# Layer 0's graph convolution in pairs of groups: four tiled mixes in a row, then the full products of two groups

## The chip, the cores and the metric

The kernel runs on one core of one Trainium2 chip. Its engines are TensorE (PE in the profile: matmuls; PEld are its weight loads), VectorE (DVE), ScalarE (ACT), GpSimd (POOL) and SyncE (SP), which issues most DMAs; each works through its own queue in order. Matmul results land in PSUM, which has eight banks here, and VectorE or ScalarE must copy them out. The metric is the device time of one execution in microseconds (us), lower is better.

## The reference, cut to what matters

Four layers, each of them `x = x + layer(relu(layernorm(x)))`, on x of 128 batches, 64 nodes and 256 features in f32; the same 64 x 64 adjacency serves all. Layer 0, which the change touches, is a graph convolution of two steps followed by LSTMs over windows of nodes:

```python
h = relu(layernorm(x))                                        # kernel's "h"
h = relu(einsum('ts,bsh->bth', adj, h @ Wg0 + bg0))           # first step
h = relu(einsum('ts,bsh->bth', adj, h @ Wg1 + bg1))           # second step
for p in range(1, 5):                                         # LSTM p over windows of p nodes
    ...
```

The layers after it (attention, a batch-normalized network, three graph products) are not changed.

## The kernel before

**Groups.** The 8192 rows (128 batches x 64 nodes) are cut into 16 groups of 512 rows (`NG`, `GN`): 4 tiles of 128 partitions, and each tile holds two batches of 64 nodes. Every group passes four stages in layer 0. Each step first mixes the nodes with the adjacency and then multiplies by the weights; the bias goes through the adjacency's row sums.

- `first_mix(g)`, line 427: the normalization of group g (`ln_relu`, line 117: statistics L92, L94 and L95 on VectorE, a power L96 on POOL, one more L98 on VectorE, whose result is called nmr, and then four activations L111 on ScalarE write h); then `mix` (line 132), 32 matmuls of 64 x 64 (L144), which address the array as four tiles of 64 x 64. They fill two PSUM banks, and VectorE copies both to m0 (L157 and L452). `copied_of[g]` (line 425) remembers the second copy.
- `first_weights(m0)`, line 479: 8 full matmuls of 128 x 256 (L487) into two banks. For each bank VectorE adds the bias (L495) and POOL takes the relu (L496); the result is h1.
- `second_mix(h1)`, line 499: again 32 tiled matmuls (L144) into two banks; ScalarE copies both to m1 (L157).
- `second_weights(g, m1)`, line 504: 4 full matmuls of 128 x 512 (L511) into two banks; VectorE adds the bias (L516), ScalarE takes the relu (L519) and writes into `hs`, which the LSTMs read.

The profile counts each f32 matmul twice: a mix is x64, a first weights x16, a second weights x8.

**Order of the stages (lines 522 to 532).** One loop, software-pipelined: in turn g it issues the first mix of g, the second weights of g-2, the second mix of g-1 and the first weights of g. So on TensorE a mix always stands between two stages of full products, except at the two ends of the loop. At the end, the second weights of group 14 are split around the second mix of 15.

**What sets the order on the other engines.** The program is written stage by stage, and a scheduler merges the engines' instructions by what they wait for. `tc.issue_after(...)` holds an instruction behind another one in the program. In `first_mix` it holds the normalization of group g behind `copied_of[g - 2]` (line 447), and `ln_relu` gets a function, `lambda: copied_of[g - 1]` (line 448), that holds its last small operation L98 behind the copy of the group before. Other work is hung on the same list: sums of LSTM weights (L226) and differences of finished groups (L214) behind `copied_of[5]` to `copied_of[15]`, and the forms of the adjacency (L374 to L397) behind the mix of group 4.

**Buffers.** All PSUM tiles come from one ring of eight banks (`psp`, line 47). h, m0, h1, m1 and s1 have two buffers each (`gp`, line 321). The groups from 4 on load x into three buffers (line 445) through SP's queue, which also carries the LSTM weights of 1 MB each (L318).

**After the loop** the LSTMs start on TensorE (L568) with products of 128 x 256, of which the first read groups 0 to 7.

Of the kernel before, what the change touches and what calls it, by code (L numbers as in the profile page):

```python
# [20 lines left out]
NG = NTOK // GN  # L21
# [17 lines left out]
def adj_preln_kernel(ctx: ExitStack, tc: tile.TileContext, x_in, adj, vec, bg0, bg1,  # L39
# [9 lines left out]
    def bank(shape=(P, 512)):  # L49
        return psp.tile(list(shape), F32, tag="ps", name="ps")  # L50
# [6 lines left out]
    def load_x(x, g):  # L57
        nc.sync.dma_start(out=x, in_=x_view[:, g * GT : (g + 1) * GT, :])
# [25 lines left out]
    def ln_scale(src, between=None, n=GT, early=False):  # L84


        st = lnp.tile([P, GT, 6], F32, tag="st", name="st")[:, 0:n]
        mv = lnp.tile([P, GT, 2], F32, tag="mv", name="mv")[:, 0:n]
        rstd = lnp.tile([P, GT], F32, tag="rstd", name="rstd")[:, 0:n]
        nmr = lnp.tile([P, GT], F32, tag="nmr", name="nmr")[:, 0:n]  # L90
        for t in range(n):
            nc.vector.bn_stats(st[:, t, :], src[:, t, :])  # L92
        for t in range(n):
            nc.vector.bn_aggr(mv[:, t, :], st[:, t, :])  # L94
        var = nc.vector.tensor_scalar(rstd, mv[:, :, 1], LN_EPS, None, ALU.add)  # L95
        nc.gpsimd.tensor_tensor(out=rstd, in0=rstd, in1=mhalf[:, 0:n], op=ALU.pow)  # L96
        with tc.issue_after(between().ins) if between else nullcontext():
            last = nc.vector.scalar_tensor_tensor(nmr, mv[:, :, 0], -1.0, rstd, ALU.mult, ALU.mult)  # L98
        return rstd, nmr, (var if early else last).ins

    def ln_apply(src, dst, rstd, nmr, n=GT, on_vector=()):

        for t in range(n):
            if t in on_vector:
                nc.vector.tensor_scalar(
                    dst[:, t, :], src[:, t, :], rstd[:, t : t + 1], nmr[:, t : t + 1],
                    ALU.mult, ALU.add,
                )
                last = nc.vector.tensor_scalar(dst[:, t, :], dst[:, t, :], 0.0, None, ALU.max)
                continue  # L110
            last = nc.scalar.activation(  # L111
                dst[:, t, :], src[:, t, :], AF.Relu,
                bias=nmr[:, t : t + 1], scale=rstd[:, t : t + 1],
            )
        return last.ins

    def ln_relu(src, dst, between=None):

        rstd, nmr, _ = ln_scale(src, between)
        ln_apply(src, dst, rstd, nmr)  # L120
# [193 lines left out]
    with tc.tile_pool(name="lw", bufs=5) as lw:  # L314
# [6 lines left out]
        with tc.tile_pool(name="gw", bufs=1) as gw, tc.tile_pool(name="gcn", bufs=2) as gp, \  # L321
# [103 lines left out]
            copied_of = []  # L425

            def first_mix(g):
                nonlocal first_copied, first_scalar, turned, second_ln
                h = gp.tile([P, GT, D], F32, tag="h", name="h")
                if g == 0:  # L430
                    for k, (rstd, nmr, _) in enumerate(lns):
                        two = slice(2 * k, 2 * k + 2)
                        ln_apply(xs[0][:, two], h[:, two], rstd, nmr, 2, (1,) if k else ())
                elif g == 1:
                    with tc.issue_after(first_copied):
                        rstd, nmr, second_ln = ln_scale(xs[1])
                    with tc.issue_after(first_scalar):
                        ln_apply(xs[1], h, rstd, nmr)
                    with tc.issue_after(first_copied):
                        row_sums()  # L440
                else:
                    if g < NK:
                        x = xs[g]
                    else:
                        x = gp.tile([P, GT, D], F32, tag="x", name="x", bufs=3)
                        load_x(x, g)
                    with tc.issue_after(second_ln if g == 2 else copied_of[g - 2].ins):
                        ln_relu(x, h, lambda: copied_of[g - 1])
                m0 = gp.tile([P, 2, GN], F32, tag="m0", name="m0")

                def on_vector_last(*args):
                    copied_of.append(nc.vector.tensor_copy(*args))  # L452
                    return copied_of[-1]

                if g == 0:


                    def on_scalar_first(*args):
                        nonlocal first_scalar
                        last = nc.scalar.copy(*args)  # L460
                        first_scalar = last.ins
                        return last

                    copied = mix(h, adj2, 2, m0, (on_scalar_first, on_vector_last))
                    first_copied = copied
                    with tc.issue_after(copied):
                        nc.vector.tensor_scalar(rb0[:, 0, :], rb0[:, 0, :], rsum, None, ALU.mult)
                else:
                    copied = mix(h, adj2, 2, m0, (on_vector, on_vector_last))
                if g == NG // 4:  # L470

                    with tc.issue_after(copied):
                        adjacency_forms()
                        turned = normalized_adjacency()
                if g == NG // 2:
                    turned()
                return m0

            def first_weights(m0):

                h1 = gp.tile([P, GT, D], F32, tag="h1", name="h1")
                for k in range(2):
                    ps = bank((P, 2, D))
                    for t in range(2):
                        tok = (2 * k + t) * P
                        for c in range(2):
                            nc.tensor.matmul(  # L487
                                ps[:, t, :],
                                lhsT=m0[:, c, tok : tok + P],
                                rhs=wg[0][:, c, :],  # L490
                                start=(c == 0),
                                stop=(c == 1),
                            )
                    hk = h1[:, 2 * k : 2 * k + 2, :]
                    nc.vector.tensor_tensor(hk, ps, rb0.to_broadcast([P, 2, D]), ALU.add)  # L495
                    nc.gpsimd.tensor_scalar(hk, hk, 0.0, None, ALU.max)  # L496
                return h1

            def second_mix(h1, last):
                m1 = gp.tile([P, 2, GN], F32, tag="m1", name="m1")  # L500
                mix(h1, adj2, 2, m1, (on_scalar, on_vector if last else on_scalar))
                return m1

            def second_weights(g, m1, ms=range(2)):

                dst = hs[g // PER][:, :, :, (g % PER) * GB : (g % PER + 1) * GB]
                for m in ms:
                    ps = bank((P, GB, NODES))
                    pf = ps.rearrange("p b n -> p (b n)")
                    for c in range(2):  # L510
                        nc.tensor.matmul(  # L511
                            pf, lhsT=wg[1][:, c, m * P : (m + 1) * P], rhs=m1[:, c, :],
                            start=(c == 0), stop=(c == 1),
                        )
                    s1 = gp.tile([P, GB, NODES], F32, tag="s1", name="s1")
                    nc.vector.tensor_tensor(  # L516
                        s1, ps, rb1[:, m].to_broadcast([P, GB, NODES]), ALU.add
                    )
                    nc.scalar.activation(dst[:, m], s1.rearrange("p b n -> p n b"), AF.Relu)  # L519


            h1, m1 = None, None
            for g in range(NG + 2):
                if g < NG:
                    m0 = first_mix(g)
                before = m1
                if before is not None:
                    second_weights(g - 2, before, range(1 if g == NG else 2))
                m1 = second_mix(h1, g == NG) if h1 is not None else None
                if g == NG:  # L530
                    second_weights(g - 2, before, [1])
                h1 = first_weights(m0) if g < NG else None


        with tc.tile_pool(name="back", bufs=1, reuse_waits="tile") as back_pool, \
# [198 lines left out]
            for p, nk in ((1, 8), (2, 8), (3, 7), (4, 8)):  # L734
                n = nk * HB
# [6 lines left out]
                for j in range(0, len(units), 2):  # L742
# [23 lines left out]
                    for t in range(1, p):  # L766
                        for i, u in enumerate(two):
# [21 lines left out]
                            if p == 4 and j == 2 and t == p - 1 and i == 0:  # L789

                                h = back_pool.tile([P, GT, D], F32, tag="hc", name="h")
# [10 lines left out]
    def arena(pool):  # L802
        return pool.tile([P, 4, GN], F32, tag="arena", name="arena")
# [47 lines left out]
    with tc.tile_pool(name="att", bufs=2, reuse_waits="tile") as ap_:  # L851
# [151 lines left out]
        for g in range(NG):  # L1003
# [14 lines left out]
            if g == 0:  # L1018
                h = normalized(1)
# [51 lines left out]
            with tc.issue_after(sub):  # L1071
# [4 lines left out]
                if g + 2 < NG:  # L1076
                    h = normalized(g + 2)
# [493 lines left out]
    for g in range(NG + 1):  # L1571
        if g == 0:
            bring(0, 3)
        if g < NG:

            m1 = arena(ar_right)
            h1, summed = first_weights(a, m1)
# [89 lines left out]
```

## Time and profile before

| what | value |
|---|---|
| median of 4 runs | 2450.08 us (2449.26 to 2452.09) |
| the profiled execution | 2452.09 us, its span 2450.20 us |
| first matmul of the mix of group 2 | 22.92 us from the span's start |
| first matmul of the LSTMs (L568) | 163.85 us |
| TensorE in the stretch 20 to 140 us | busy 20.00 us of every 20 |
| VectorE there | 12.86 to 14.49 us of every 20 |
| ScalarE there | 10.06 to 12.56 us of every 20 |
| POOL there | 8.08 to 9.10 us of every 20 |
| granted TensorE clock, 20 us and later | 1.00 |

The profile is that of one execution. In the list of groups each row names line, engine, operation, what it writes and reads, the shape, the count, the busy time and the mean duration in ns, and after the last bar how long the engine stood idle before such instructions and who ended that. A timeline merges neighbours of one kind: start, duration of the whole row, engine, line, operation, the part of the array (64*64 or 128*128 for a matmul), shape, count. In both, `[a <-b]` says that the engine was idle for a us until b released it. The ends of matmuls are modelled and neighbours overlap by some hundredths to tenths of a us, so the pace of TensorE is read from one start to the next.

### The profile page before, as it was taken

The numbers are of one execution on the slowest core, as the hardware profiler recorded it, in microseconds if no ns is written. First come the engines' busy times: TensorE is split into PE (matmuls) and PEld (weight loads), VectorE is DVE, ScalarE is ACT, GpSimd is POOL, SyncE is SP. The second block draws the span as 40 slices with busy tenths as digits, with TensorE's granted clock in tenths as the row PEclk, the third lists the DMA queues.
The fourth block names the chain that finished last, engine by engine and source line by source line (L and its number), as shares of the span: only waits on it lengthen the run. The fifth ranks groups of instructions, "written<-read, shape, count | busy, mean of one in ns | idle before, by whom it ended". The sixth has DMA issues, their size and how long they took to land.

```text
span 2450.2 us, 46580 instructions
## 1 busy us (share of the span) xinstructions
PE 2429.6 (99%) x19564; PEld 2073.1 (85%) x19564; DVE 1541.3 (63%) x2768; ACT 1128.0 (46%) x2026; POOL 463.6 (19%) x400
## 2 busy tenths in 40 slices
PE   9999999999999999999999999999999999999999
PEld 6678888889999998888888864486988898898888
DVE  6668866656566575575698886476555445454544
ACT  4557754544445344353455566564333323333332
POOL 4432211111111111112234331023111111111110
PEclk9999999999999999999999999999999999999999
DMA  3200000001000000153246410010133100000000
GB/s 123 99 2 1 1 18 1 1 1 35 1 1 1 1 1 1 18 100 69 48 87 121 79 35 2 1 61 10 34 54 62 27 10 19 10 10 10 18 10 18
DMA packets 161586, 73.20 MB, mean 30 GB/s; under 512 B 104416, under 2 KB 157792, under 8 KB 161376
## 3 DMA queue, kind: packets, MB, share of 16 engines
q1 hardware_dynamic: 147712, 56.82, 9.4%
q0 software_dynamic: 12672, 12.58, 3.4%
q8 instruction: 154, 2.52, 0.4%
q10 hardware_dynamic: 992, 0.82, 0.1%
q14 instruction: 56, 0.46, 0.1%
HBM read 40.84 MB, written 20.97 MB: 25 GB/s over the span
## 4 chain that ended last, share of the span: by engine, by line
PE 90%; DVE 6%; ACT 3%; POOL 1%; issue 1%; DMA 0%; DVEq 0%; POOLq 0%; ACTq 0%
PE ps L568 41%; PE ps L1454 16%; PE ps L1502 8%; PE ps L830 4%; PE ps L144 4%; PE ps L880 3%; PE ps L1418 2%; PE ps L511 2%; PE ps L487 2%; PE ps L1210 2%; PE ps L1261 2%; PE ps L902 1%; ACT arena L237 1%; POOL arena L187 1%; PE ps L963 1%
## 5 line engine op out<-in xcount | busy, mean ns | idle before, releaser
L568 PE MATMUL ps<-diff,s 128*128 128x256 f32 (+1 forms) x1824 | 393.5, 371 | 0.9 <-DVE diff L689 0.9
L1454 PE MATMUL ps<-arena 128*128 128x256 f32 x1792 | 392.6, 381 | 0.0
L1454 PEld LDWEIGHTS ps<-arena 128*128 128x128 f32 x1792 | 337.9, 190 | 54.2 <-issue 9.5
L568 PEld LDWEIGHTS ps<-diff,s 128*128 128x128 f32 x1824 | 345.9, 190 | 33.8 <-issue 1.6
L582 ACT ACTIVATE gates<-gates,lbias 128x512 f32<-128x512 f32 (+5 forms) x426 | 244.2, 620 | 200.5 <-DVE gates L193 144.4
L187 POOL TENSOR_TENSOR gates<-p 128x512 f32<-128x512 f32 (+1 forms) x115 | 148.8, 1294 | 881.8 <-DVE p L183 831.0
L568 PE MATMUL ps<-h,w 128*128 128x256 f32 (+1 forms) x1028 | 241.0, 371 | 0.0
L568 PE MATMUL ps<-diff,w 128*128 128x256 f32 (+1 forms) x1040 | 238.7, 370 | 0.0
L568 PEld LDWEIGHTS ps<-diff,w 128*128 128x128 f32 x1040 | 197.4, 190 | 18.2
L568 PEld LDWEIGHTS ps<-h,w 128*128 128x128 f32 x1028 | 195.0, 190 | 19.2 <-issue 0.5
L582 ACT ACTIVATE gates<-ps,lbias 128x256 f32<-128x256 f32 (+3 forms) x213 | 91.8, 477 | 247.5 <-PE ps L568 247.4
L187 POOL TENSOR_TENSOR arena<-arena 128x256 f32<-128x256 f32 (+1 forms) x73 | 81.8, 1121 | 580.5 <-DVE arena L183 550.9
L237 ACT ACTIVATE arena<-arena 128x512 f32<-128x512 f32 (+1 forms) x160 | 88.6, 582 | 187.0 <-POOL arena L187 94.8
L1502 PE MATMUL ps<-arena 128*128 128x128 f32 x1280 | 149.7, 276 | 0.0
L193 DVE TENSOR_TENSOR gates<-p,ps 128x512 f32<-128x512 f32 (+1 forms) x115 | 76.3, 664 | 114.4 <-PE ps L568 114.2
L1502 PEld LDWEIGHTS ps<-arena 128*128 128x128 f32 x1280 | 145.5, 192 | 1.1
L193 DVE TENSOR_TENSOR arena<-arena,ps 128x256 f32<-128x256 f32 (+1 forms) x73 | 43.6, 597 | 156.0 <-PE ps L1454 87.4
L568 PE MATMUL ps<-state,w 128*128 128x256 f32 (+1 forms) x512 | 116.1, 370 | 0.9 <-ACT p L179 0.8
L182 DVE TENSOR_TENSOR p<-p,ps 128x512 f32<-128x512 f32 (+1 forms) x131 | 86.8, 663 | 47.9 <-PE ps L568 46.8
L197 DVE TENSOR_TENSOR gates<-p,ps 128x512 f32<-128x512 f32 (+1 forms) x115 | 76.6, 666 | 63.3 <-PE ps L568 62.7
L830 PE MATMUL ps<-arena,w 128*128 128x512 f32 x256 | 116.0, 606 | 0.0
L568 PE MATMUL ps<-state,s 128*128 128x256 f32 (+1 forms) x512 | 115.8, 369 | 0.0
(207 smaller groups left out, 4022.2 us busy)
## 6 DMA issues: line engine op xcount, KB each, us to landing
x<-in_x SPq DMA_DIRECT2D x19, 512.0 KB, 4.9
y<-turned SPq DMA_DIRECT2D x64, 128.0 KB, 3.7
v<-vt SPq DMA_DIRECT2D x128, 64.0 KB, 2.3
w<-in_wih SPq DMA_DIRECT2D x4, 1024.0 KB, 8.4
x_for_h<-in_x SPq DMA_DIRECT2D x8, 512.0 KB, 7.5
x<-y POOLq DMA_DIRECT2D x8, 512.0 KB, 6.1
x_for_h<-y POOLq DMA_DIRECT2D x8, 512.0 KB, 6.7
z<-w SPq DMA_DIRECT2D x64, 64.0 KB, 2.0
```

What stands on the lines that cost most here:

```text
L144: last = nc.tensor.matmul(pss[b][half * 64 : half * 64 + 64, c, t, :], lhsT=src[rows, t, col : col + 64], rhs=a2[rows, :], start=True, sto ...
L182: nc.vector.tensor_tensor(p1, p1, ps[2], ALU.add)
L187: nc.gpsimd.tensor_tensor(out=out[1][1], in0=p1, in1=p5, op=ALU.add).ins
L193: nc.vector.tensor_tensor(out[0][1], p1, ps[1], ALU.add)
L197: last = nc.vector.tensor_tensor(to, p, q, ALU.add)
L237: nc.scalar.activation(o, o, func)
L568: nc.tensor.matmul(ps[:, r], lhsT=wc[:, j, :], rhs=bc, start=first and r == 0 and c == 0, stop=True, skip_group_check=True,)
L582: nc.scalar.activation(o, ps, func, bias=lbias[:, col : col + 1])
L830: nc.tensor.matmul(ps, lhsT=w1[:, c, m * P : (m + 1) * P], rhs=a[:, 2 + c, :], start=(c == 0), stop=(c == 1),)
L880: nc.tensor.matmul(ps[:, r, :], lhsT=w[:, r * P : (r + 1) * P], rhs=x, start=first and r == 0, stop=True, skip_group_check=True,)
L1454: nc.tensor.matmul(ps[:, r, :], lhsT=w[:, c, col : col + P], rhs=b[:, c, :], start=first and r == 0 and c == 0, stop=c == 1, skip_group_ch ...
L1502: nc.tensor.matmul(ps[:, t, :], lhsT=w[:, c, t * P : (t + 1) * P], rhs=b[:, c, :], start=first and t == 0 and c == 0, stop=c == 3, skip_gr ...
```

## The change

Groups 2 to 15 are taken in pairs. For a pair g, g+1 the order is: first mix of g, second mix of g-2, first mix of g+1, second mix of g-1; then first weights of g, second weights of g-2, first weights of g+1, second weights of g-1. In the pair 14, 15 both first weights stand ahead of both second weights. So a second mix and its weights stand two groups behind, where they stood one and two. Groups 0 and 1 keep their order, the pair 2, 3 has no second mix of 0 (it is done before), and after the loop come the second mixes of 14 and 15 and then their second weights. `copied_of[g - 1 - g % 2]` makes L98 of an odd group wait for the copy of the pair before, not for that of its own pair's first group. The first of the two copies of m1 stays on ScalarE; the second goes to VectorE for groups 14 and 15, where it was for 15 alone.

```diff
--- before.py
+++ after.py
@@ -445,7 +445,7 @@
                         x = gp.tile([P, GT, D], F32, tag="x", name="x", bufs=3)
                         load_x(x, g)
                     with tc.issue_after(second_ln if g == 2 else copied_of[g - 2].ins):
-                        ln_relu(x, h, lambda: copied_of[g - 1])
+                        ln_relu(x, h, lambda: copied_of[g - 1 - g % 2])
                 m0 = gp.tile([P, 2, GN], F32, tag="m0", name="m0")
 
                 def on_vector_last(*args):
@@ -519,17 +519,36 @@
                     nc.scalar.activation(dst[:, m], s1.rearrange("p b n -> p n b"), AF.Relu)
 
 
-            h1, m1 = None, None
-            for g in range(NG + 2):
-                if g < NG:
-                    m0 = first_mix(g)
-                before = m1
-                if before is not None:
-                    second_weights(g - 2, before, range(1 if g == NG else 2))
-                m1 = second_mix(h1, g == NG) if h1 is not None else None
-                if g == NG:
-                    second_weights(g - 2, before, [1])
-                h1 = first_weights(m0) if g < NG else None
+            h1_of, m1_of = [], []
+
+            def first_weights_of(m0):
+                h1_of.append(first_weights(m0))
+
+            def second_mix_of(g):
+                m1_of.append(second_mix(h1_of[g], g >= NG - 2))
+
+            for g in range(2):
+                m0 = first_mix(g)
+                if g:
+                    second_mix_of(0)
+                first_weights_of(m0)
+            for g in range(2, NG, 2):
+                m0s = []
+                for n in range(g, g + 2):
+                    m0s.append(first_mix(n))
+                    if n > 2:
+                        second_mix_of(n - 2)
+                for n in range(2):
+                    first_weights_of(m0s[n])
+                    if g + 2 < NG:
+                        second_weights(g - 2 + n, m1_of[g - 2 + n])
+                if g + 2 == NG:
+                    for n in range(2):
+                        second_weights(g - 2 + n, m1_of[g - 2 + n])
+            for n in range(NG - 2, NG):
+                second_mix_of(n)
+            for n in range(NG - 2, NG):
+                second_weights(n, m1_of[n])
 
 
         with tc.tile_pool(name="back", bufs=1, reuse_waits="tile") as back_pool, \
```

## The prediction

> **What bounds the kernel now.** The page first: parts 1 and 2 say which engine is full and at what clock.
>
> ```profile
> PE 2429.6 (99%) x19564; PEld 2073.1 (85%) x19564; DVE 1541.3 (63%) x2768; ACT 1128.0 (46%) x2026; POOL 463.6 (19%) x400
> ...
> PEclk9999999999999999999999999999999999999999
> ```
>
> TensorE is busy 99% of the span at full clock. The chain of waits says the same: TensorE 90%. The change touches layer 0's graph products, which are 64 columns wide (L144, "mix") or full (L487 first weights, L511 second weights). So next I read TensorE's timeline through them; its columns are start, duration, line, tile of the array, shape, count. The time that a stage takes from the path is the distance to the next start, not the duration, since matmuls overlap.
>
> ```profile
> 22.92 1.16 PE L144 MATMUL ps<-adj,h 64*64 64x64 f32 x64
> ...
> 104.57 3.72 PE L487 MATMUL ps<-wg,m 128*128 128x256 f32 x16
> 108.22 1.16 PE L144 MATMUL ps<-adj,h 64*64 64x64 f32 x64
> 109.31 3.70 PE L511 MATMUL ps<-m,wg 128*128 128x512 f32 x8
> 112.95 1.16 PE L144 MATMUL ps<-adj,h 64*64 64x64 f32 x64
> 114.04 3.72 PE L487 MATMUL ps<-wg,m 128*128 128x256 f32 x16
> ...
> 155.46 1.88 PE L511 MATMUL ps<-m,wg 128*128 128x512 f32 x4
> 157.26 1.40 PE L144 MATMUL ps<-adj,h 64*64 64x64 f32 x64
> 158.59 5.42 PE L511 MATMUL ps<-m,wg 128*128 128x512 f32 x12
> 163.85 1.03 PE L568 MATMUL ps<-h,w 128*128 128x256 f32 x4
> 164.71 2.75 PE L568 MATMUL ps<-diff,s 128*128 128x256 f32 x12
> 167.30 1.03 PE L568 MATMUL ps<-h,w 128*128 128x256 f32 x4
> ```
>
> A group costs 114.04 - 104.57 = 9.47 us, with no idle time in it: 3.65 (L487), 1.09 (mix), 3.64 (L511), 1.09 (mix). Nothing there waits for another engine, so only the matmuls' own pace can be gained. Full and tiled stages alternate, and each stage runs slower than its own pace:
> - L568 is a 128x256 product among full ones: 167.30 - 164.71 = 2.59 for 12, 0.216 each. Sixteen would be 3.45; L487 takes 3.65, **0.20 more**.
> - L511: the 4 at 155.46 take 1.80 with a tiled stage only behind them, the 12 at 158.59 take 5.26 with one only ahead. Together 16 take 7.06 with one border of each kind, and 8 in the middle take 3.64 with the same two. So 8 cost 3.42, and the two borders **0.22**.
> - Tiled stages in a row are not in layer 0 undisturbed, but they are at the start of layer 2:
>
> ```profile
> 1428.37 1.16 PE L144 MATMUL ps<-ah,arena 64*64 64x64 f32 x64
> 1429.35 1.14 PE L976 MATMUL ps<-v,eT 64*64 64x64 f32 x64
> 1430.29 1.16 PE L927 MATMUL ps<-k,q 64*64 64x64 f32 x64
> 1431.38 3.70 PE L830 MATMUL ps<-arena,w 128*128 128x512 f32 x8
> ```
>
> Three stages of one shape take 0.98, 0.94, 1.09: 3.01 where three alone would take 3 x 1.09 = 3.27. Each joint between tiled stages saves **0.13**.
>
> **What the change gains.** It adds and removes no product; it only reorders. From the mix of group 2 on, there are now 14 first mixes and 15 second mixes, each standing alone: 29 tiled runs. After, by the program's own order, they are one run of three (groups 2, 3 and the second mix of 1), six of four, one of two: 8 runs. That is 21 joints of tiled stages and 21 of full ones: 21 x (0.13 + 0.21) = **7.1 us**. A pair of groups goes from 18.94 to 3.95 (four mixes: 0.98 + 0.94 + 0.94 + 1.09) + 13.95 = 17.9 us. Bounds of the joint: in layer 3, the last 96 tiled matmuls of a mix that had waited ran at 1.52 us, 0.0158 each, so 64 cost 1.01 and a joint only 0.07 to 0.08, and the gain is 21 x 0.28 = 5.9; in another place of layer 2 a last mix took 1.04, a joint is 0.15, the gain 7.6. I take 0.13, the row with the same shapes, three in a row.
>
> **What the start loses.** TensorE's cover at the start is gone: between the mix of 2 (22.92) and the next ones stood 3.6 us of L511. POOL's timeline of the same stretch shows what is then late:
>
> ```profile
> 21.36 1.01 POOL L96 TENSOR_TENSOR rstd<-rstd,mhalf 128x4 f32<-128x4 f32 x1 [2.15 <-DVE rstd L95]
> 22.34 2.95 POOL L496 TENSOR_SCALAR h<-h 128x512 f32<-128x512 f32 x2
> ```
>
> L96 is group 3's power, L496 the relu that finishes h1 of group 1. The nmr of group 3 (L98) no longer waits for copies of group 2 and now stands ahead of the two additions L495 of group 1 on DVE's queue. It waits for POOL until 22.4, so the additions, now 21.30 and 23.03, end at 23.2 and 23.85, and the relus at 24.75 and 26.25 (it was 25.29). ScalarE applies group 3 from 22.65, 2.1 us for four (L111), so its mix follows to 25.05. The second mix of 1 has its first half then, and waits for the second until 26.25; the full products start at 26.8 where an unhindered run of three would end at 22.92 + 3.01 = 25.93. **Loss 0.9 us**, between 0.4 (additions not held up) and 1.5.
>
> **What the steady pairs need.** Rows of layer 0 between 25 and 150 us, count, then busy and mean ns:
>
> ```profile
> L496 POOL TENSOR_SCALAR h<-h 128x512 f32<-128x512 f32 x27 | 40.2, 1490 | 21.4 <-DVE h L495 21.3
> ...
> L92 DVE BATCH_NORM_STATS2 st<-x 128x6 f32<-128x256 f32 x48 | 17.9, 414 | 0.0
> ...
> L96 POOL TENSOR_TENSOR rstd<-rstd,mhalf 128x4 f32<-128x4 f32 x12 | 12.4, 1033 | 47.2 <-DVE rstd L95 47.2
> L452 DVE COPY m<-ps 128x512 f32<-128x512 f32 x14 | 9.5, 681 | 0.0
> ```
>
> Count from the start of mix g. TensorE: mixes to 3.95; L487 of g to 7.5; L511 of g-2 to 10.95; L487 of g+1 to 14.4; L511 of g-1 to 17.9. DVE in its order: the last addition L516 to 0.7; two copies of m0 of g (0.68 each) from 1.05 to 2.4; a normalization (four L92 in 1.40, L94 0.36, a weight sum L226 0.66, L95 0.17) to 5.0; copies of m0 of g+1 to 6.4; the second normalization to 9.2; its nmr waits for the power to 10.5, and L495 of g queue behind it: to 11.9; L516 to 13.3; L495 of g+1 to 15.1; L516 at 16.8 and 18.6. POOL's relus: g 11.3 to 14.3, g+1 14.3 to 17.3. They are wanted by the mixes at 18.9 and 20.8: **4.6 and 3.5 us to spare**. In the pair of groups 4 and 5 the adjacency forms (L374 to L397, some 13 small operations and one wait for POOL) push the relu of 5 to 19.7, 1.1 to spare. ScalarE copies m1 of g-1 only behind a normalization's first activations, at about 8.7; L511 wants it at 14.4. PSUM: the four mixes take all eight banks, and L487 of g takes the two of its mix again at 3.95, free at 2.4. SP: x of g+3 takes the buffer of x of g, free once its L111 is done, in the pair before; 4.9 us to land against over 10 us of room; the 1 MB weight loads still go between and are not wanted before the LSTM. So I cost the steady pairs at **nothing**; without that cover each microsecond is paid seven times.
>
> The Trainium skill speaks against this ("TensorEngine Tiling (Array Packing)", Performance Considerations, PSUM Bottleneck): tiling speeds up the matmuls and not the emptying of PSUM, so that the copies can become the bound. Here eight copies come due within 3.95 us; four on DVE are 4 x 0.68 = 2.7 us, four on ScalarE (L157, 0.58) 2.3. By the rule the run of full products would wait for DVE's last copy at 6.4, 2.45 us in each of 7 pairs, 17 us; by the rows it needs only the first two, at 2.4. I follow the rows.
>
> **The tail.** The second mix of 15 now loses 0.24 us (157.26 to 158.59 is 1.33). After, L511 of 14 waits for a copy of its m1 on ScalarE, which stands behind the last L519 of group 13 (1.09): about 0.45. Loss 0.2.
>
> **Sum:** 7.1 - 0.9 - 0.2 = **6.0 us**. The profiled execution took 2452.09 us (span 2450.20 and 1.89 around it), so it would take 2446.1. It is the longest of the four before; against their median of 2450.08 the forecast is **2444.1 us**.
>
> **Rivals.**
> - *Small waits eat part of it*, 26%: the joint is worth 0.08 (5.9 - 1.1 = 4.8), or relus come late at the second mix. For: POOL's relus come in a burst of four, 6 us, behind DVE's two waits for powers. Against: 3.5 us to spare. With 0.3 us lost per pair, 2.1 in all, 2446.2; with 0.6, 2448.3.
> - *Eviction decides, slower*, 6%: DVE reaches the copies of m0 of g late, because the next normalization stands ahead with its wait for the power (2.6 + 1.1 us). They then end at 6.1 instead of 2.4, L487 starts 2.15 late, 7 x 2.15 = 15; net 9 slower, **2459**. It decides once they end after 5.0, where the 1.04 gained per pair is gone. Against: DVE's order as built has these copies first.
> - *Borders vanish better*, 4%: 0.36 per joint and no start loss, 7.6, 2442.5 or below.
>
> **Numbers.** The forecast's own case, a gain of 4.9 to 7.6, has 64%. A measurement of this kernel tells about 0.2% (4.9 us) from no change. So faster 0.68, same 0.26, slower 0.06. The range takes in the bounds of the joint (5.9 to 7.6), of the start, a scatter of 1 us, and most of the first rival: 2441.5 to 2448.5.
>
> **What would show it.** In the profile after: TensorE's timeline with runs of 256 tiled matmuls of 3.9 to 4.0 us, then 13.95 us of full ones without idle time; pairs 17.9 us apart; the first full products after group 3's mix at about 26.8; L568 starting near 157.8 (163.85 before). Wrong if: the tiled run has gaps that wait for L496 or L111, L487 waits for DVE's copies, or a joint saves less than 0.28 in all.

## The result, and the profile after

The changed kernel takes **2452.66 us** (median of 41 runs, 2451.10 to 2455.03) against 2449.92 (median of 61 runs of the kernel before, beside it on the same chips): 1.0011 times, with a 95% interval of 1.0006 to 1.0015. The forecast was 2444.1 with a range to 2448.5. So the change costs 2.7 us where a gain of 6.0 was forecast, and the 8.7 us between the two are to be found. The profiled execution took 2452.69 us, close to the median.

The page of the changed kernel, parts 1 to 4, first: the lines that answer to those shown of the kernel before, and one on a DMA queue that matters below.

```profile
PE 2422.6 (99%) x19564; PEld 2073.0 (85%) x19564; DVE 1541.4 (63%) x2769; ACT 1129.8 (46%) x2025; POOL 463.2 (19%) x400
...
PEclk9999999999999999999999999999999999999999
...
q8 instruction: 154, 2.52, 0.4%
...
PE 89%; DVE 6%; ACT 3%; POOL 1%; issue 1%; DMA 0%; DVEq 0%; POOLq 0%; ACTq 0%
```

The number of TensorE's instructions is unchanged and so is its mean granted clock (0.999 in both), but it is busy 7.0 us less (2422.6 for 2429.6) in a span that is 0.7 us longer than that of the profiled execution before. So it stands idle 7.7 us more. Its timeline through layer 0 shows where (the LSTM's L568 is L587 in this kernel, since the change adds 19 lines ahead of it):

```profile
21.72 3.05 PE L144 MATMUL ps<-adj,h 64*64 64x64 f32 x160
25.31 0.69 PE L144 MATMUL ps<-adj,h 64*64 64x64 f32 x32 [0.54 <-POOL h L496]
25.93 3.72 PE L487 MATMUL ps<-wg,m 128*128 128x256 f32 x16
...
39.90 3.71 PE L144 MATMUL ps<-adj,h 64*64 64x64 f32 x237
44.64 0.56 PE L144 MATMUL ps<-adj,h 64*64 64x64 f32 x19 [1.03 <-issue]
45.13 3.72 PE L487 MATMUL ps<-wg,m 128*128 128x256 f32 x16
...
59.10 3.02 PE L144 MATMUL ps<-adj,h 64*64 64x64 f32 x188
65.14 1.83 PE L144 MATMUL ps<-adj,h 64*64 64x64 f32 x68 [3.02 <-issue]
66.91 4.77 PE L487 MATMUL ps<-wg,m 128*128 128x256 f32 x16
...
157.17 2.09 PE L144 MATMUL ps<-adj,h 64*64 64x64 f32 x128
159.72 7.13 PE L511 MATMUL ps<-m,wg 128*128 128x512 f32 x16 [0.46 <-ACT m L157]
166.70 1.03 PE L587 MATMUL ps<-h,w 128*128 128x256 f32 x4
```

The full products run as forecast: from 45.13 to 59.10 are 13.97 us, without a break. The runs of 256 tiled matmuls do not: five of the six are cut once, by 1.03, 3.02, 1.03, 0.80 and 0.90 us, each time in the middle of a mix, and "issue" as the releaser means that the profile knows no engine and no transfer of data that TensorE waited for. Only the run at 81.93 is whole, 4.01 us with four small products of the adjacency in it. The waits of TensorE between 25 and 160 us, where the kernel before has none at all:

```profile
PE ps L144 <- issue: 6.8, 5, 3.0
PE ps L144 <- POOL h L496: 0.5, 1, 0.5
PE ps L511 <- ACT m L157: 0.5, 1, 0.5
```

The six steady pairs, from 39.90 to the tiled run at 157.17, take 117.3 us, where the prediction's 17.9 each make 107.4 and the 18.94 of before 113.6. So **9.9 us are lost there**: 6.8 in the gaps themselves, and the rest right behind them: 0.3 in the rest of each of the four runs with a short gap (39.90 to 45.13 is 5.23, less the gap of 1.03 still 0.3 over 3.9), 0.9 in the rest of the run with the long gap, and 1.05 in the L487 after it (66.91), which takes 4.60 to the next start instead of 3.56.

These last two, 1.9 us together, have a cause of their own, which the tenths of the page are too coarse to show. Behind the long gap TensorE's granted clock is halved for some 3.4 us. Each row gives a stretch, its length, how long TensorE was busy in it and with how many matmuls, the granted clock, and the DMA share and GB/s:

```profile
63.60:65.60 2.00, 0.46 (x25) 1.00 0.00 0
65.70:69.00 3.30, 3.30 (x56) 0.50 0.02 5
69.10:71.50 2.40, 2.40 (x12) 1.00 0.14 35
```

Half the clock for 3.4 us costs up to 1.7 us (an estimate: half of 3.4). At the four short gaps the clock is 1.00 before and behind, so the gaps themselves are no matter of the clock. The gaps of 2.71 us in experiment 3 and of 2.94 in experiment 9 have such a stretch behind them too; in experiment 7, where the gap at this place is 1.09, the clock stays 1.00.

The start adds 0.3: its first run takes 4.21 instead of the forecast 3.9. One difference goes the other way and hides part of the loss. This execution reached the mix of group 2 at 21.72 us, the kernel before at 22.92, with a granted clock of 0.50 from 16.1 to 19.4 us there and of 1.00 here. Experiments 3 and 7, whose program up to that mix is the same as here, also ran such a stretch and reached the mix at 22.69 and 22.84. So these 1.2 us are scatter between executions and not a gain of the change. With them the account closes: the first LSTM product stands at 166.70 where 157.8 was forecast, 8.9 us late, and 9.9 and 0.3 less 1.2 are 9.0. (The table ahead of the prediction gives the clock before as 1.00 from 20 us on; that holds for layer 0, but from 1453.1 to 1456.4 us, long behind the change, that execution ran at 0.50 again.)

**What "issue" is here.** The queue q8 in the page carries instructions: 154 packets in 2.52 MB are 16.4 KB each. TensorE has 19564 matmuls and as many weight loads, 39128 instructions, 254 to a packet. So q8 brings TensorE its own program, in blocks of some 256 instructions, about 64 bytes each. The DMA view of the changed kernel between 100 and 105 us, in 40 slices of 0.125 us, has nothing else in it:

```profile
DMA  0000000000000040000000000000000000000000
...
q8 instruction: 1, 0.02, 1.1%
```

The block starts at 101.84 us and TensorE goes on at 104.30, 2.5 us later; for the gaps that end at 44.64 and 122.57 it is 2.4 (blocks at 42.26 and 120.15). A tiled matmul with its weight load is two instructions and takes 0.0152 us here (3.9 / 256), so a block, 128 matmuls, lasts 1.95 us in a tiled run. Among full products it lasts far longer: 96 instructions take 13.97 us.

The places of the cuts say the same. They come after 237, 188, (none), 213, 164 and 242 matmuls of the run: each 49 earlier than in the pair before, or, once that falls out of reach, 128 later than that (164 - 49 + 128 is 243). A pair has 4 x 128 instructions in its tiled run and 2 x (32 + 16) in its full products, 608, which is two blocks and 96 instructions, or 48 matmuls, one fewer than the step seen. A wait for data would stand at the same matmul in every pair.

### The profile page after: what moved, and what is told of

Its sections match the earlier page's. It is cut to its first block, busy times and chain, and to the rows that moved or that the text cites. A ratio compares the mean times of both kernels' runs of the same rounds, so it can differ in the third digit from the quotient of the medians.

```text
span 2450.9 us, 46556 instructions
## 1 busy us (share of the span) xinstructions
PE 2422.6 (99%) x19564; PEld 2073.0 (85%) x19564; DVE 1541.4 (63%) x2769; ACT 1129.8 (46%) x2025; POOL 463.2 (19%) x400
## 3 DMA queue, kind: packets, MB, share of 16 engines
q8 instruction: 154, 2.52, 0.4%
## 4 chain that ended last, share of the span: by engine, by line
PE 89%; DVE 6%; ACT 3%; POOL 1%; issue 1%; DMA 0%; DVEq 0%; POOLq 0%; ACTq 0%
PE ps L587 41%; PE ps L1473 16%; PE ps L1521 8%; PE ps L849 4%; PE ps L144 3%; PE ps L899 3%; PE ps L1437 2%; PE ps L511 2%; PE ps L1229 2%; PE ps L487 2%; PE ps L1280 2%; PE ps L921 1%; ACT arena L237 1%; POOL arena L187 1%; PE ps L982 1%
## 5 line engine op out<-in xcount | busy, mean ns | idle before, releaser
L587 PE MATMUL ps<-diff,s 128*128 128x256 f32 (+1 forms) x1824 | 393.5, 371 | 0.9 <-DVE diff L708 0.9
L587 PEld LDWEIGHTS ps<-diff,s 128*128 128x128 f32 x1824 | 345.9, 190 | 33.8 <-issue 1.6
L587 PE MATMUL ps<-h,w 128*128 128x256 f32 (+1 forms) x1028 | 241.0, 371 | 0.0
L587 PE MATMUL ps<-diff,w 128*128 128x256 f32 (+1 forms) x1040 | 238.7, 370 | 0.0
L587 PEld LDWEIGHTS ps<-diff,w 128*128 128x128 f32 x1040 | 197.4, 190 | 18.2
L587 PEld LDWEIGHTS ps<-h,w 128*128 128x128 f32 x1028 | 195.0, 190 | 19.2 <-issue 0.5
L587 PE MATMUL ps<-state,w 128*128 128x256 f32 (+1 forms) x512 | 116.1, 370 | 0.9 <-ACT p L179 0.8
L587 PE MATMUL ps<-state,s 128*128 128x256 f32 (+1 forms) x512 | 115.8, 369 | 0.0
```

What stands on the lines that cost most here:

```text
L587: nc.tensor.matmul(ps[:, r], lhsT=wc[:, j, :], rhs=bc, start=first and r == 0 and c == 0, stop=True, skip_group_check=True,)
```

## The experiments

The theory, called *fetch* below: a run of four mixes asks for 512 instructions within 3.9 us, and the blocks do not come that fast. Its rivals: *data*, a hidden wait for a copy, a bank of PSUM or an input, which four mixes in a row bring closer; and *weights alone*, that the gaps come from the 1 MB LSTM weight loads that share the DMA engines. In the edits below, a line of dots stands for what is left out.

### 1 and 2: the same mixes with a quarter of the instructions

Both kernels, the pairs and the order of before, with mixes of 8 matmuls of 64x64x256 instead of 32 of 64x64x64: the adjacency stands in the array and h streams through. The result lies otherwise in PSUM and is not turned back, so these kernels do not compute the reference's values; copies, banks, waits and multiply-adds are as many as they were.

```diff
...
+            for b in range(2):
+                rows = slice(b * 64, b * 64 + 64)
+                half = t % 2
+                nc.tensor.matmul(
+                    pss[b][half * 64 : half * 64 + 64, t // 2].rearrange("p t n -> p (t n)"),
+                    lhsT=a2[rows, :], rhs=src[rows, t, :], start=True, stop=True,
+                )
...
```

> The changed kernel, but each mix of layer 0 is 8 matmuls of 64 x 64 x 256 with the adjacency as the loaded operand, where it was 32 of 64 x 64 x 64; the same columns are streamed, banks and copies are the same, m0 and m1 hold other numbers (layout not turned), so the values are not the reference's. A run of four mixes then has 128 TensorE instructions instead of 512. Theory fetch (TensorE's instructions come in blocks of 16 KB, a run of four mixes uses them up faster than they come): the gaps of 0.8 to 3.0 us in the tiled runs vanish, runs take 3.9 to 4.0 us, L487 at 66.9 loses its extra 1.0, the whole takes 2442 to 2444. Rival data (the mixes wait for a copy, a bank or an input that the profile doesn't name): order and data flow are unchanged, the gaps stay, 2452 to 2453.

> The kernel before with the same 8 matmuls of 64 x 64 x 256 for each mix of layer 0 (values not the reference's): the control for what the form itself does. Theory fetch: before has no such gaps, so about 2449.9, within 1.5 us; a mix alone stays near 1.09. Rival data: the same. If it is faster by several us, the form and not the fetch makes the gain of the other run.

Measured: the pairs 2442.47 us, 0.9968 (0.9956 to 0.9979) of the kernel before; the old order with the same mixes 2448.29, 0.9994 (0.9984 to 1.0003), 1.6 us under the kernel before where at most 1.5 was expected. In the old order a mix alone takes 1.03 us where it took 1.09, so the shape itself is worth little. The **pairs' order gains 5.8 us** there, against 6.0 forecast for the change, and the two intervals do not overlap. The profiled execution of the first kernel took 7743 us and is not read; the same kernel was profiled again.

> The changed kernel with mixes of 8 matmuls of 64 x 64 x 256 again (values not the reference's), for its profile, since the profiled execution of the first was disturbed. Theory fetch: runs of 64 matmuls without a gap, 3.9 us or less, no extra 1.0 in any L487 (line numbers moved). Rival data: gaps of about 1 us in the runs.

That execution took 2442.41 us. The TensorE timeline of the quarter pairs, and TensorE's waits from 25 to 160 us:

```profile
40.98 3.69 PE L166 MATMUL ps<-h,adj 64*64 64x256 f32 x64
44.60 3.72 PE L502 MATMUL ps<-wg,m 128*128 128x256 f32 x16
...
58.57 3.69 PE L166 MATMUL ps<-h,adj 64*64 64x256 f32 x64
```

```profile
PE ps L526 <- ACT m L172: 0.6, 1, 0.6
PE ps L166 <- POOL h L511: 0.4, 1, 0.4
```

Four mixes in a row, 3.62 us, no gap, and a pair takes 17.59. The two waits that are left are those that the prediction had, the start's and the tail's. *Data* falls here: the runs are faster than those of the changed kernel, so each copy, bank and input is wanted earlier, and none is late.

### 3: the weight loads later, by an order on POOL

Two of the LSTM weight loads stand on SP's queue just ahead of the long gap. This kernel was to send them only after the second relu of group 6.

```diff
...
-                    w_next = (load_w(wih, p), load_w(whh, p))
+                    w_next = (load_w(wih, p, relus[13] if p == 2 else None), load_w(whh, p, relus[13] if p == 1 else None))
...
```

> The changed kernel with two of the LSTM weight loads of 1 MB (whh of 1, wih of 2) held behind the relu of group 6, so that they no longer move at 55 to 63 us, beside the run of four mixes at 59.1. Theory fetch: a block of instructions queues behind them there; the gap of 3.0 in that run becomes about 1.0 like the other ones, which stay, and the extra 1.0 of L487 after it goes: 2449.5 to 2450.5. Rival weights alone (all gaps come from the loads): the gaps of 0.8 to 1.0 elsewhere go too. Rival data: nothing changes, 2452 to 2453.

Measured: 2453.49 us, 1.0014 (1.0004 to 1.0023). It **failed as an experiment**, as SP's timeline shows:

```profile
55.28 0.51 SPq L319 DMA_DIRECT2D w<-in_whh  x1
```

The other goes at 55.83; in the changed kernel they go at 54.52 and 55.07. `issue_after` put the loads behind the relu in the written program, but SP did not wait for POOL by it: that relu runs at 72 to 75 us, and SP's own queue had nothing ahead of the loads. So the loads did not move, and the gaps came back in the same runs (1.63, 2.71, none, 1.36, 1.07, 1.18), the short ones 0.3 to 0.6 us longer: a second sample of the changed kernel, no more.

### 4: two mixes in a row instead of four

One group at a time: first mix of g, second mix of g-2, second weights of g-3, first weights of g. A tiled run then has 256 instructions. L98 waits for the copy of the group before, as it did; the rest is the changed kernel's.

```diff
...
+            for g in range(NG):
+                m0 = first_mix(g)
+                if g >= 2:
+                    second_mix_of(g - 2)
+                if g >= 3:
+                    second_weights(g - 3, m1_of[g - 3])
+                first_weights_of(m0)
...
```

> Not pairs but single groups with two mixes in a row: first mix of g, second mix of g-2, then second weights of g-3 and first weights of g. 16 tiled runs instead of 29 standing alone, 13 joints of 0.34 us. A run has 256 TensorE instructions. Theory fetch: one block covers a run, no gaps, 13 x 0.34 = 4.4 less a loss of 0 to 1 at the start: 2445.5 to 2446.5, 9.1 us a group. Rival data (mixes wait when second mixes stand two groups behind or when four banks are taken in a row): gaps of 0.5 or more per run, 2450 or more.

Measured: 2448.13 us, 0.9994 (0.9984 to 1.0003), slower than the 2445.5 to 2446.5 expected. No "issue" gap in layer 0, and a group takes 9.11 us where it took 9.47. The whole of TensorE's waits there is `PE ps L487 <- DVE m L452` with 2.4 us, twice, at the start (1.85 and 0.54), which takes back a good part of the 14 x 0.36. Behind the longer wait the granted clock is 0.50 from 18 to 21 us.

### 5 and 6: mixes of half the instructions

Mixes of 16 matmuls that use 128 columns (64x128 of the array), so that a run of four has 256 instructions; again in the pairs and in the order of before.

```diff
...
+                    nc.tensor.matmul(
+                        pss[b][:, c, t, :], lhsT=src[rows, t, c * P : (c + 1) * P],
+                        rhs=a2[rows, :], start=True, stop=True,
+                    )
...
```

> The changed kernel with the same values, but each mix of layer 0 as 16 matmuls of 64 x 128 x 64 (all 128 features of h loaded at once) where it was 32 of 64 x 64 x 64. A run of four mixes has 256 TensorE instructions instead of 512. Theory fetch: at most one border of a 16 KB block is met early in a run, so no gap, or one of a few tenths; if the form keeps its 0.94 us a mix, 2443 to 2445. If loading 128 columns for 64 streamed ones takes longer (a mix of 1.2 or more), the form costs 29 x 0.3 = 9 and the gaps go all the same: 2451. Rival data: the gaps stay at 0.8 to 3.0, 2452 or more.

> The kernel before with mixes of 16 matmuls of 64 x 128 x 64: the control for the form. Both theories: 2449.9 within 1.5 if a mix alone stays at 1.09; 2455 or more if the loads of 128 columns show.

Measured: 2470.15 us (1.0077, 1.0060 to 1.0094) and 2475.59 (1.0104, 1.0088 to 1.0119). This form of the mix is far slower in itself than either case expected, 1.93 us alone instead of 1.09, so it is no test of half the instructions at the same speed. The first line is of the half pairs, the second of its control:

```profile
45.20 7.36 PE L166 MATMUL ps<-adj,h 64*128 64x64 f32 x128
```

```profile
104.08 2.00 PE L166 MATMUL ps<-adj,h 64*128 64x64 f32 x32
```

What it does show: 256 instructions in 7.29 us (to 52.49) come without a gap, and the pairs' order again gains, 5.4 us by the medians, though here the two intervals touch.

### 7: the weight loads behind an x load, on SP's own queue

The hold that failed, made with an instruction that SP itself issues.

```diff
...
-                    w_next = (load_w(wih, p), load_w(whh, p))
+                    w_next = (load_w(wih, p, first_loads[11] if p == 2 else None), load_w(whh, p, first_loads[11] if p == 1 else None))
...
```

> The changed kernel with the two LSTM weight loads of 1 MB put behind the load of x of group 11 on SP's own queue, which stands still until about 70 us, so that they really leave the stretch 55 to 63 us (the run before this one only moved them in the program and not in time). Theory fetch with a queue of DMA work ahead of the block: in the run of four at 59 to 67 us the gap falls from 2.7 to 3.0 to about 1.0 to 1.5, the second one of 1.0 in L487 behind it goes, the other runs keep theirs; 2449.5 to 2450.5. Theory fetch without that queue, or rival data: nothing changes, 2452 to 2453.5.

Measured: 2450.78 us, 1.0004 (0.9994 to 1.0013), 0.3 above the 2449.5 to 2450.5 expected. Now the loads go at 69.90 and 72.57. TensorE's timeline of that kernel (L144 is L146 there, L487 is L490):

```profile
41.03 3.71 PE L146 MATMUL ps<-adj,h 64*64 64x64 f32 x237
45.75 0.56 PE L146 MATMUL ps<-adj,h 64*64 64x64 f32 x19 [1.01 <-issue]
...
60.22 3.02 PE L146 MATMUL ps<-adj,h 64*64 64x64 f32 x188
64.32 1.29 PE L146 MATMUL ps<-adj,h 64*64 64x64 f32 x68 [1.09 <-issue]
65.54 3.72 PE L490 MATMUL ps<-wg,m 128*128 128x256 f32 x16
```

The long gap has shrunk from 3.02 to 1.09 us, and its place, after 188 matmuls, is the same. The L487 after it, which took 4.60 us to the next start in the changed kernel, takes its 3.56 again, at a granted clock of 1.00. The other gaps stay (1.01, 0.97, 0.80, 0.84), and one of 0.18 comes among full products, at 85.26. So *weights alone* falls: the loads made one gap 2 us longer, with the halved clock behind it, and made none of the others. How they did that is in the DMA view of the changed kernel from 60 to 66 us, in slices of 0.15 us:

```profile
DMA  9999999999999998320400000000000000000000
...
q8 instruction: 1, 0.02, 1.0%
```

All engines are full until 62.3, and the one block of instructions comes at 62.86, when the weights are through; TensorE stands from 62.12 to 65.14.

### 8: two mixes in a row, with the start covered

Two mixes in a row as in 4, but groups 2 and 3 keep the second weights of groups 0 and 1 between their mixes, so that the start is covered as in the kernel before, and the second mixes of 14 and 15 stand in one run behind the second weights of 13.

```diff
...
+            for g in range(2, NG):
+                m0 = first_mix(g)
+                if g < 4:
+                    second_weights(g - 2, m1_of[g - 2])
+                    if g == 2:
+                        second_mix_of(1)
+                else:
+                    second_mix_of(g - 2)
+                    if g > 4:
+                        second_weights(g - 3, m1_of[g - 3])
+                first_weights_of(m0)
...
```

> The order with two mixes in a row (first of g, second of g-2; then second weights of g-3, first weights of g), but with the start as in the kernel before up to group 2, one group of transition, and both last second mixes in one run behind the second weights of 13. Tiled runs of 256 TensorE instructions, no work left out. Theory fetch: no gaps in the tiled runs; 9.11 us a group as in the run of the same order before it, about 12 joints of 0.34 us, and less lost at the start than there (1.8): 2446 to 2447.2. Rival: if the start costs as much as it did, or a block border in a run still stalls, 2448 or more.

Measured: **2446.32 us** (2445.69 to 2448.57) against 2450.14, 0.9985 (0.9976 to 0.9994), within what was expected: a small gain, but faster than both kernels. Its TensorE timeline, and the waits from 15 to 160 us:

```profile
45.51 2.10 PE L144 MATMUL ps<-adj,h 64*64 64x64 f32 x128
47.53 3.70 PE L511 MATMUL ps<-m,wg 128*128 128x512 f32 x8
51.07 3.62 PE L487 MATMUL ps<-wg,m 128*128 128x256 f32 x16
```

```profile
PE ps L487 <- DVE m L452: 0.7, 2, 0.5
PE ps L511 <- ACT m L157: 0.5, 1, 0.5
PE ps L144 <- POOL h L496: 0.4, 1, 0.4
```

A tiled run takes 2.02 us and holds 256 instructions, one block; no wait of it is unnamed.

### 9: the gaps brought back where there were none

The order of 8, with every matmul of layer 0's mixes, but for the first mix of group 0, issued twice into the same place.

```diff
...
-                        for b in range(2):
+                        for b in [*range(2)] * times:
...
```

> Order, copies and data flow of e9_two_mixes_start, whose runs of two mixes (256 TensorE instructions) had no gap. From group 1 on every matmul of a mix is issued twice into the same place of PSUM, with the same operands, so the values stay the same and nothing else moves; a run of two mixes now has 512 instructions, as a run of four in the changed kernel. Fetch: the gaps come back although only two banks pairs and two mixes' inputs are in play: about 1 us, charged to no engine, in four of five tiled runs, at a place that moves back by about 24 matmuls from group to group (560 instructions a group, 48 over two blocks of 256). A group then takes 9.11 + 2 x 0.94 + about 0.8 = 11.8 us. Data (a copy, a bank or an input that the run of four waits for): no gaps, 9.11 + 1.88 = 11.0 us a group. In all the kernel is slower by 14 x 1.9 to 14 x 2.7, some 27 to 38 us more than e9, by construction.

Measured once: 2495.43 us beside 2449.59 of the kernel before. That is 49 us above experiment 8, where 27 to 38 was expected; 14.6 of them are the waits below, and the extra matmuls make most of the rest. TensorE's timeline, and its waits from 15 to 190 us:

```profile
130.92 4.01 PE L144 MATMUL ps<-adj,h 64*64 64x64 f32 x256
...
141.94 3.71 PE L144 MATMUL ps<-adj,h 64*64 64x64 f32 x234
146.75 0.67 PE L144 MATMUL ps<-adj,h 64*64 64x64 f32 x22 [1.09 <-issue]
...
154.44 3.31 PE L144 MATMUL ps<-adj,h 64*64 64x64 f32 x209
159.23 0.97 PE L144 MATMUL ps<-adj,h 64*64 64x64 f32 x47 [1.48 <-issue]
```

```profile
PE ps L144 <- issue: 14.6, 11, 2.9
```

The gaps are back, 0.7 to 1.5 us in four of the five runs from 130.92 to 179.31, and they move back by 25 matmuls from group to group, as 560 instructions a group (two blocks and 48, 24 matmuls) would have it. The four groups in that stretch take 12.1 us each, against 11.8 expected by *fetch* and 11.0 by *data*. Neither the quarter pairs nor this run changes the number of instructions alone: the first also swaps the loaded operand and the streamed one, and here the multiply-adds double. But copies, banks and inputs are the same in both, and the gaps follow the number of instructions in both directions. That is shown; what is inferred is how the block is asked for. In the first cut run of the changed kernel TensorE passes its 109th matmul, one block ahead of the gap, at about 41.6 us, and the packet starts at 42.26: it comes soon after TensorE has passed into the block before. The one whole run there (81.93) is the one whose block came early, at 78.06, because the border before it fell into the first matmuls of the run (the 11th, by the step of 49) and was reached, by the part of TensorE that reads ahead, among the slow full products.

## Why the prediction was wrong, point by point

**The failed step is "What the steady pairs need", and its end: "So I cost the steady pairs at nothing".** It listed what the pairs need of VectorE, POOL, ScalarE, PSUM and SP's queue, and for each of them it was right: in six pairs no named wait. It left out what TensorE needs by itself, its instructions. The loss is 1.1 to 1.3 us in each of four pairs and 4.9 in the one that meets the weight loads (a gap of 3.0 and up to 1.7 of halved clock behind it), 9.9 us in all, where nothing stood in the sum. The prediction had written that "without that cover each microsecond is paid seven times"; it was paid five times.

By terms:

| term of the sum | forecast | measured |
|---|---|---|
| a stretch of four stages of full products | 13.95 us | 13.97 |
| a run of four mixes | 3.95 | 3.9 in the run without a gap; 5.0 to 5.2 in four of the others, 7.8 in the fifth |
| 21 joints of both kinds | 7.1 | 7.4, from 0.20 and 0.15 a joint (below) |
| loss at the start | 0.9 | 1.2 (4.21 for the run, 3.01 unhindered), in an execution that came to it 1.2 early by scatter |
| wait ahead of the tail's L511 | 0.45 | 0.46 |
| the steady pairs | 0 | 9.9 |
| net, order alone, with few instructions | 6.0 | 5.8 and 5.4 |

- **The joints** were right in size. The rows they came from hold for this kernel: 13.97 for 14.58 (twice 3.65 + 3.64) is 0.61 for three joints of full products, 0.20 each (0.21 forecast); four mixes in 3.9 instead of 4.36 are 0.15 a joint (0.13).
- **The start.** The second mix of 1 waited for its relu on POOL, as described, 0.54 us of it as a visible wait, and 0.3 us more was lost than forecast. A size, and a small one.
- **PSUM.** The prediction held the rows against the Trainium skill ("TensorEngine Tiling (Array Packing)", Performance Considerations, PSUM Bottleneck). The runs side with the rows: no L487 of the steady pairs waits for a copy of VectorE, even in the quarter pairs, where it comes 0.3 us sooner. Waits for such copies were seen only where a run of mixes was followed by its own first weights with little ahead of them: 0.26 us at 18.07 in the changed kernel, 0.7 in all in experiment 8, and 2.4 us of `PE ps L487 <- DVE m L452` at the uncovered start of experiment 4.
- **The rivals.** "Small waits eat part of it" had the right kind of case, a loss in each pair, but the price of 0.3 or 0.6 us a pair was too small and the mechanism (late relus) was not it. "Eviction decides, slower" had the right sign and did not happen. None of them named the instruction supply.
- **Where it could have been read.** The page of the kernel before has the same 154 packets on q8. In layer 0 it had used at most 256 instructions of tiled matmuls in a row, once, and slowly (3.9 us):

```profile
15.21 3.97 PE L144 MATMUL ps<-adj,h 64*64 64x64 f32 x128 [1.91 <-ACT h L111]
```

  The three stages of layer 2 are 384 in 3.0 us; 512 in 3.9 us was nowhere in the rows that it read. The prediction took the pace of three stages (192 matmuls, layer 2) for that of four, without asking what else 512 instructions in a row need.

The Trainium skill does have the mechanism ("Runtime: NRT & Kernel Launch", Instruction fetch mechanics): an engine's instructions are refilled in blocks of 16 KiB, 256 instructions, over a DMA queue of its own while the block before is used up, and crossing a border is "mostly hidden". The trace agrees on the block (16.4 KB, 256 instructions) and, but for 0.18 us in experiment 7, on the hiding wherever full products stand between; at 1.95 us a block it does not: the changed kernel's trace shows 0.8 to 1.0 us a border, and 3.0 where data fills the DMA engines.

What stays open: why the short gaps differ by tenths from run to run (1.03 in the changed kernel's first, 1.63 in that of experiment 3), how long a gap must be for the clock to be halved behind it, and whether a gap depends on how the blocks lie by chance. A few instructions more or less ahead of layer 0 move the borders, and the one run in six that escaped here would be another one.

## What to carry to other kernels

Count the instructions of a stretch against its time, not only its products: where small matmuls follow each other so that 512 instructions of TensorE last 3.9 us, as here, it can run out of program, and the profile then shows idle time charged to "issue", at a place that wanders with the block's border. Reordering that gathers small stages is worth its saved borders only as long as the blocks keep up; here runs of two mixes (256 instructions, one block) gained 3.8 us and runs of four lost 2.7, and steady runs of three were not tried. A larger matmul per instruction (64x256 for 64x64, a quarter of the instructions at the same time) took the gaps away; what it would cost to turn its result back was not measured. And a gap of 3 us can cost more than itself, so read the granted clock behind it.

## What the runs showed of the hardware that was not expected

- TensorE's instructions come in blocks of 256 by DMA, and in the changed kernel's gaps TensorE goes on 2.3 to 2.5 us after the block's packet starts. They share the DMA engines with data: with two 1 MB loads under way a gap was 3.02 us, with these elsewhere 1.09.
- Behind gaps of 2.71, 2.94 and 3.02 us (experiments 3 and 9 and the changed kernel) TensorE's granted clock is 0.50 for some 3.4 us; behind the gaps of 0.8 to 1.6 us in the pairs it stays 1.00.
- The mix as 64x128 tiles with 64 columns streamed takes 1.93 us alone, as 64x64 tiles 1.09, and with 256 columns streamed 1.03: half as many matmuls took 1.8 times as long, a quarter as many a little less.
- An order between two engines in the written program (`issue_after` on an instruction of POOL) did not hold a DMA on SP's queue; one on SP's own queue moved two by 15 and 17 us.
